# A three-layer graph network on one core: the first layer's neighbour lists are analysed first, and its row gathers are dealt by estimated time

## The chip, the cores and the metric

The kernel runs on one core of a Trainium2 chip. The metric is device time in microseconds (us) of one execution. The engines are named as in the profile: PE (TensorE), DVE (VectorE), ACT (ScalarE), POOL (GpSimd) and SP (the queue that issues most plain DMAs).

## The reference

There are 6250 nodes with 128 features and 200000 edges, sorted by destination. After a layer norm and a ReLU come three layers of the same form (widths 128 to 256, 256 to 256, 256 to 128), and the input is added at the end:

```python
def _sage_conv(x, src, dst, Wl, bl, Wr):
    agg = jax.ops.segment_max(x[src], dst, num_segments=x.shape[0])
    agg = jnp.where(jnp.isfinite(agg), agg, 0.0)
    return agg @ Wl + bl + x @ Wr
h = jnp.maximum(_layernorm(x, axis=-1), 0.0)
for Wl, bl, Wr in layers:
    h = jax.nn.leaky_relu(_sage_conv(h, src, dst, Wl, bl, Wr), 0.01)
return x + h
```

Nearly all work is in `segment_max(x[src], dst)`: for every node, the maximum over its neighbours' rows.

## The kernel before

The nodes form 50 tiles of 127 rows. The neighbours of a node are taken in two ways. Of the neighbours that lie in one pair of source tiles, one (or two) is taken by **lookup**: a one-hot matrix is made from a row of indices and multiplied on PE with the pair of source tiles. What is left over goes to **lists**: at most some tens of neighbours of a node, fetched row by row from the table in DRAM by indirect DMAs that POOL issues (a **gather**: 128 rows of 128 floats in the first layer).

**Steps.** The three layers are written as 1025 steps; the first layer is steps 0 to 224. In the code it is `layer == 0`; the text calls it the first layer. It has three sweeps over the 25 pairs of source tiles: steps 0 to 74 take the lookups of group 0 (three steps for each pair), steps 75 to 124 those of group 1 (two steps for each pair), steps 125 to 224 those of groups 2 and 3 (four steps for each pair). In a step PE makes the products (`products`, L997), and DVE takes the running maximum over them out of PSUM (`maxima`, L1014). The one-hots are made up to six steps ahead. In the first sweep all of them are made on ACT (L967 and L969); in the two others ACT makes one half and DVE the other (L963).

**Chores.** The lists and the index rows have to be made from the edges first. Group 0 and list 0 are done before step 0. For lists 1, 2 and 3 this is work for DVE during the first layer's steps: `late_rows(k)` masks and flags the rows of a list (`mask_rows`, `flag_rows` with `repeated`), picks what is left over (`pick_rows`, L558 and L560) and ranks the rows by their count (`rank_rows`, from L574). POOL then scatters the picked rows, one indirect DMA each (`send_row`, L630), and SP loads the ordered list (`load_ell`). `late_lookups(us, s)` makes the index rows for the lookups (`expand`, L742 to L749, and `lookups`). `spread` deals the chores over the steps in proportion to a cost written by hand.

**Gathers.** `CAPS` says how many gathers each column of a list takes: 118 for list 0, 70, 255 and 110 for lists 1, 2 and 3, so 553 in a layer. 44 of the first layer's are issued before step 0 (`early`). `release` copies four index columns on ACT (`let`, L1035), `gather` issues on POOL (L1046) into a ring of 8 tiles, each of 8 gathers in the first layer, and `maximum` takes the maximum of the tiles on DVE (L1060, then a tree, L1065) and sends a column's result to `best` by a DMA on SP's queue (L1069). Where each stands is set by `plan(step, rank, f)`: every engine takes its instructions in the order of the steps, and within a step in the order of ranks. Before the change the gathers that are left after the early ones are dealt evenly over the layer's steps, and the maximum stands eight steps (four for list 3) behind the gather:

```python
for part, t0, t1 in (((items[:parted], t0, turn), (items[parted:], turn, t1)) if alone else ((items, t0, t1),)):
    ...
    while total[t + 1] <= total[-1] * i / n:
        t += 1
    whens.append(t0 + t)
...
plan(max(whens[i] - LEAD, 0), LET, lambda li=li, t=t: li.release(t))
plan(whens[i], GATHER, lambda li=li, t=t: li.gather(t))
at = max(at, whens[i] + (SOON if k == NL - 1 and not (alone and i < parted) else DELAY[layer]))
plan(at, MAXIMA, lambda li=li, t=t: li.maximum(t))
```

**Nodes.** When a group's sweep and its list are done, each of its tiles is finished (`Node`): POOL fetches the list's maximum (L1089; L1158 for the split rows of group 1), PE transposes it and multiplies by the weights, and the new rows go to the next layer's table. The next layer's gathers begin when the whole table is written.

Of the kernel before, what the change touches and what calls it, by code (L numbers as in the profile page):

```python
# [66 lines left out]
HOT, HOTS, MORE = 1024, 6, 1  # L67
# [5 lines left out]
def kernel(ctx: ExitStack, tc: tile.TileContext, x, src, dst,  # L73
# [32 lines left out]
    LISTS = ([("n", i) for i in range(NEAR)],) + GROUPS[1:]  # L106
# [6 lines left out]
    NL = len(LISTS)  # L113
# [308 lines left out]
    jobs = []  # L422
# [7 lines left out]
    for i in range(NEAR):  # L430
        window(ORDER[i])
        while rest and len(jobs) - 4 - len(rest) <= i * (len(jobs) - 4) / 17:
            stage, b = rest.pop(0)
# [194 lines left out]
    def send_row(k, i):  # L628
        nc.gpsimd.memset(gap_t, 0.0)
        s = nc.gpsimd.indirect_dma_start(  # L630
            out=picks[k], out_offset=bass.IndirectOffsetOnAxis(ap=to_i[k][:, i : i + 1], axis=0),
            in_=picked[k][:, i, :], in_offset=None,
        )
        for j in sent[k]:
            tc.declare_no_dep(s.ins, j.ins, reason="rows are disjoint")
        sent[k].append(s)

    def load_ell(k):
        n = len(LISTS[k])
        nc.sync.dma_start(ell[k], picks[k].rearrange("(p q) m -> p q m", q=n))  # L640
# [217 lines left out]
    for (f, k), s in best.items():  # L858
        n = len(LISTS[k]) * P
# [34 lines left out]
    RING = 8  # L894
# [252 lines left out]
    class Joined:  # L1147
# [27 lines left out]
        def send(self, v):  # L1175
            K, F = self.K, self.F
            p = psum.tile([P, K, P], F32, tag="tr", name="jT_p")
            for i in range(K):
                nc.tensor.transpose(p[:, i, :], self.acc[:, i, v * P : (v + 1) * P], ident)
            t = node.tile([P, H], F32, tag="s", name="joined_v", bufs=2)  # L1180
            nc.scalar.copy(t[:, :F], p.rearrange("p k f -> p (k f)"))
            nc.sync.dma_start(joined[F][v * P : (v + 1) * P, :], t[:, :F])


    steps, begins, ends_at = [], [], {}
# [24 lines left out]
    def plan(t, rank, f):  # L1210
        agenda.setdefault((t, rank), []).append(f)

    LET, TURN, MAXIMA, ROWS, REST, LINEAR, MERGE, SOONER, GATHER, FETCH = range(10)
    LEAD = 2
# [7 lines left out]
    chores = []  # L1222
    here_now, listed_at = [0], {0: 0}

    def late_rows(k):
        us = LISTS[k]
        i0 = 0
        for part in [list(p) for _, p in itertools.groupby(us, key=lambda u: u[0])]:
            chores.append((2.5, lambda part=part: mask_rows(part, S_acc)))
            chores.append((len(part) * (1 if part[0][0] == "w" else .6), lambda part=part: flag_rows(part, S_acc)))  # L1230
            for i in range(0, len(part), 4):
                chores.append((7, lambda k=k, i0=i0 + i, p=part[i : i + 4]: pick_rows(k, i0, p, S_acc)))
            i0 += len(part)
        chores.append((7, lambda: rank_rows(k, S_acc, made)))
        for i in range(0, len(us), 4):
            chores.append((0, lambda i=i: [send_row(k, j) for j in range(i, min(i + 4, len(us)))]))

        def load():
            load_ell(k)
            listed_at[k] = here_now[0]  # L1240

        chores.append((0, load))

    def late_lookups(us, s):
        got = {}
# [5 lines left out]
            chores.append((.7 * len(us), part))  # L1251
        chores.append((2, lambda: lookups(us, got[0], s, made)))

    late_rows(1)
    late_lookups(LISTS[1], 0)
    late_lookups(LISTS[1], 1)
    late_lookups(EXTRA, 0)
    n_soon = len(chores)
    late_rows(2)
    for s in range(2):  # L1260
        late_lookups(LISTS[2][:NW], s)
    rest2 = LISTS[2][NW:]
    cuts = -(-len(rest2) // 8)
    for i in range(cuts):
        late_lookups(rest2[len(rest2) * i // cuts : len(rest2) * (i + 1) // cuts], 0)
    late_rows(3)
    late_lookups(LISTS[3], 0)

    def spread(jobs, t0, t1):
        whole, done = sum(c for c, _ in jobs), 0.0  # L1270
        for c, f in jobs:
            plan(t0 + int((t1 - t0) * done / whole), MAXIMA, f)
            done += c

    spread(chores[:n_soon], 0, 40)
    spread(chores[n_soon:], 40, 82)
    DELAY = (8, 6, 6)
    SOON = 4
    WIDER = (1.0, 1.25, 1.25)
# [2 lines left out]
    for layer in range(3):  # L1282
        b0, end = begins[layer], begins[layer + 1]
        lists_ = [early_list if (layer, k) == (0, 0) else Listed(layer, k) for k in range(NL)]
        early = 0 if layer else EARLY
        turn = ends_at[layer, 2] - DELAY[layer]
        whens = []
        t0, t1 = max(b0 + 2, rows_at), end - 1 - SOON
        alone = len(SWEEPS[layer][-1]) == 1
        items = [(k, t) for k in range(NL) for t in range(len(lists_[k].seq))]  # L1290
        if alone:
            own = [(3, t) for t in range(len(lists_[3].seq))]
            later_n = len(items) * (t1 - turn) / (t1 - t0)
            heads = [t for t, (_, j) in enumerate(lists_[3].seq) if j == 0]
            cut = min(heads, key=lambda t: abs(len(own) - t - later_n))
            mid = next(i for i, (k, _) in enumerate(items) if k == 2)
            items = items[:mid] + own[:cut] + [q for q in items if q[0] == 2] + own[cut:]
            parted = len(items) - (len(own) - cut)
        for part, t0, t1 in (((items[:parted], t0, turn), (items[parted:], turn, t1)) if alone else ((items, t0, t1),)):
            total = [0.0]  # L1300
            for t in range(t0, t1):
                total.append(total[-1] + (WIDER[layer] if steps[t][3][3] is not None else 1.0))
            n = len(part) - early
            whens += [None] * early
            early, t = 0, 0
            for i in range(n):
                while total[t + 1] <= total[-1] * i / n:
                    t += 1
                whens.append(t0 + t)
        done_at, at = [0] * NL, 0  # L1310
        for i, (k, t) in enumerate(items):
            li = lists_[k]
            if whens[i] is None:
                at = 1 + i // 8
            else:
                plan(max(whens[i] - LEAD, 0), LET, lambda li=li, t=t: li.release(t))
                plan(whens[i], GATHER, lambda li=li, t=t: li.gather(t))
                at = max(at, whens[i] + (SOON if k == NL - 1 and not (alone and i < parted) else DELAY[layer]))
            plan(at, MAXIMA, lambda li=li, t=t: li.maximum(t))
            done_at[k] = at  # L1320
        gap = (2, 3, 3)[layer]
        late = 0

        def begin(key, make):
            def f():
                accs[key] = make()
                accs[key].fetch()
            return f

        def stages(ta, key, make, after=(3, 4, 5, 6)):  # L1330
            plan(ta, FETCH, begin(key, make))
            for d, rank, stage in (
                (after[0], MERGE, "merge"), (after[1], LINEAR, "linear"),
                (after[2], ROWS if after[2] > after[1] else SOONER, "rows"), (after[3], TURN, "turn"), (after[3], REST, "rest"),
            ):
# [426 lines left out]
```

## Time and profile before

| | |
|---|---|
| median of 3 runs | 3156.43 us (3152.08 to 3160.95) |
| profiled execution | 3156.75 us, span of the profile 3155.0 us, granted TensorE clock 0.914 |
| busy, of the span | PE 2407.1, DVE 2523.6, ACT 1901.4, POOL 2049.3 us |
| gathers (L1046) | 1659 in three layers, 1697.4 us on POOL |

The first layer's gathers start at 213.7 us and its last step's maxima end at about 1161 us. A row of a view gives the engine, the line, the operation, the tiles (written `<-` read), the count, the busy time with the mean of one, and the idle time ahead of it with what ended that wait. "issue" is idle time for which the profile shows no wait. PE's busy time says little on how hard it works, since matmuls are pipelined; DVE and ACT begin an instruction slightly ahead of the end of the one before, so that single durations add up to a little more than the elapsed time.

### The profile page before, as it was taken

What the parts mean: (1) busy time and instruction counts of PE and PEld (TensorE: products, weight loads), DVE (VectorE), ACT (ScalarE), POOL (GpSimd) and SP (SyncE); (2) the same over time, 40 slices, a digit from 0 to 9 for tenths busy, and PEclk for the clock granted to TensorE, in tenths of its full rate; (3) what the DMA queues carried; (4) which work ended last, traced back from release to release, by engine and by line L of the source; (5) the groups of instructions that cost most, each with busy time, mean ns of one, the idle gap of its engine ahead of it and who ended that gap; (6) DMA issues with size and microseconds to landing.
All of it is one profiled execution on the core that took longest, in us unless ns stands there. A gap on an engine that the chain in (4) does not pass through costs nothing.

```text
span 3155.0 us, 36991 instructions
## 1 busy us (share of the span) xinstructions
PE 2407.1 (76%) x9909; PEld 1806.9 (57%) x9909; DVE 2523.6 (80%) x4059; ACT 1901.4 (60%) x2793; POOL 2049.3 (65%) x2059
## 2 busy tenths in 40 slices
PE   1024643568677569999987899999999996898886
PEld 1023322345455457777775677777777775676665
DVE  7576899889778666899986679995799987799854
ACT  4216963848567556666654567874666664567652
POOL 4787543667777752677776557762477777677662
PEclk9996766779888889999998999999999998999998
DMA  9224541569566657667675676766667676776684
GB/s 299 73 60 117 158 115 54 153 146 283 167 181 179 142 148 243 203 211 216 203 183 173 220 220 209 210 201 211 209 209 219 215 176 177 212 221 205 202 254 148
DMA packets 365615, 585.57 MB, mean 186 GB/s; under 512 B 64588, under 2 KB 216279, under 8 KB 364757
## 3 DMA queue, kind: packets, MB, share of 16 engines
q1 hardware_dynamic: 237141, 336.67, 33.3%
q0 software_dynamic: 84992, 212.22, 27.2%
q10 hardware_dynamic: 43264, 34.21, 3.3%
q8 instruction: 83, 1.36, 0.2%
q14 instruction: 135, 1.11, 0.1%
HBM read 458.31 MB, written 124.54 MB: 185 GB/s over the span
## 4 chain that ended last, share of the span: by engine, by line
PE 33%; DVE 26%; DMA 16%; issue 9%; POOL 7%; ACT 5%; SPq 1%; DVEq 0%; ACTq 0%; POOLq 0%
PE pg L997 25%; DVE acc L1014 11%; DMA g<-table,let 8%; POOL g L1046 6%; PE z_p L1118 3%; DVE g L1065 3%; DVE g L1060 3%; ACT away L967 2%; PE z_p L1120 2%; ACT hot L969 2%; DMA pair_sb<-pair 1%; DVE acc L560 1%; DMA hT_in<-across 1%; DVE acc L558 1%; PE hT_p L872 1%
## 5 line engine op out<-in xcount | busy, mean ns | idle before, releaser
L997 PE MATMUL pg<-hot,pair_sb 128*128 128x512 f32 x8000 | 2113.5, 416 | 383.0 <-DVE acc L1014 108.0
L1046 POOL DMA_INDIRECT g<-table,let x1659 | 1697.4, 1023 | 677.4 <-issue 383.2
L997 PEld LDWEIGHTS pg<-hot,pair_sb 128*128 128x128 f32 x8000 | 1532.9, 200 | 834.9 <-ACT hot L969 229.9
L1014 DVE TENSOR_TENSOR acc<-acc,pg 128x1024 f32<-128x1024 f32 (+2 forms) x1239 | 1434.0, 1182 | 296.0 <-PE pg L997 278.9
L969 ACT ACTIVATE hot<-away 128x1024 fp32r<-128x1024 uint8 (+2 forms) x600 | 574.1, 957 | 350.8 <-PE pg L997 338.4
L969 ACT ACTIVATE hot<-idx_sb 128x1024 fp32r<-128x1024 uint8 (+2 forms) x600 | 555.8, 937 | 232.6 <-PE pg L997 221.9
L967 ACT ACTIVATE away<-idx_sb,near 128x1024 uint8<-128x1024 uint8 (+2 forms) x600 | 620.4, 1034 | 49.9 <-DMA idx_sb<-idx 27.1
L1060 DVE TENSOR_TENSOR g<-g 128x1024 f32<-128x1024 f32 (+5 forms) x247 | 249.3, 1009 | 63.3 <-DMA g<-table,let 56.3
L1089 POOL DMA_INDIRECT agg<-best,end_i x141 | 143.1, 1015 | 213.4 <-PE aT_p L1105 146.9
L1122 ACT COPY s<-z_p 127x256 f32<-127x256 f32 (+1 forms) x150 | 50.2, 335 | 286.0 <-PE z_p L1120 236.1
L1065 DVE TENSOR_TENSOR g<-g 128x256 f32<-128x256 f32 (+3 forms) x357 | 176.9, 496 | 10.5
L1035 ACT ACTIVATE let<-ell 128x4 int32<-128x4 int16 (+3 forms) x477 | 86.5, 189 | 103.2 <-DMA ell<-picks 92.5
L1118 PE MATMUL z_p<-wr,hT_in 128*128 128x256 f32 (+1 forms) x500 | 135.6, 389 | 3.7 <-DMA hT_in<-across 3.7
L630 POOL DMA_INDIRECT picks<-picked,to_i x55 | 56.6, 1029 | 98.4 <-DVE rank_h L606 60.5
L1120 PE MATMUL z_p<-wl,mz 128*128 128x256 f32 (+1 forms) x500 | 117.2, 351 | 2.2 <-DVE mz L1111 2.1
L1111 DVE TENSOR_TENSOR mz<-acc,aT_p 128x256 f32<-128x256 f32 (+1 forms) x141 | 52.4, 372 | 81.5 <-PE aT_p L1105 81.5
L963 DVE TENSOR_SCALAR hot<-idx_sb,beyond 128x1024 fp32r<-128x1024 uint8 (+2 forms) x150 | 108.8, 725 | 0.0
L1120 PEld LDWEIGHTS z_p<-wl,mz 128*128 128x128 f32 x500 | 88.0, 202 | 12.4 <-DVE mz L1111 3.3
L1118 PEld LDWEIGHTS z_p<-wr,hT_in 128*128 128x128 f32 x500 | 80.4, 202 | 24.9 <-DMA hT_in<-across 5.3
L353 POOL DMA_INDIRECT win_d<-in_dst_dram,win_i x50 | 52.3, 1047 | 51.3 <-ACT junk_w L358 22.7
L874 ACT COPY hT<-hT_p 128x254 f32<-128x254 f32 x100 | 36.8, 368 | 72.5 <-PE hT_p L872 71.6
L1105 PE MATMUL aT_p<-ident,agg 128*128 128x128 f32 x250 | 54.4, 284 | 22.7 <-DMA agg<-best,end_i 14.2
(284 smaller groups left out, 1109.7 us busy)
## 6 DMA issues: line engine op xcount, KB each, us to landing
pair_sb<-pair SPq DMA_DIRECT2D x325, 256.0 KB
idx_sb<-far SPq DMA_DIRECT2D x50, 640.0 KB
g<-table,let POOLq DMA_INDIRECT x1659
far<-away ACTq DMA_DIRECT2D x200, 128.0 KB
pair<-pr SPq DMA_DIRECT2D x100, 256.0 KB
idx_sb<-idx SPq DMA_DIRECT2D x75, 320.0 KB
idx_sb<-far SPq DMA_DIRECT2D x50, 320.0 KB
best<-g SPq DMA_DIRECT2D x110, 128.0 KB
```

The costliest lines, as they stand in the source:

```text
L963: nc.vector.tensor_scalar(hot[:, :w], d, beyond, None, op0=OP.is_equal)
L967: nc.scalar.activation(away, d, AF.Abs, bias=near[:, s : s + 1], scale=1.0)
L969: nc.scalar.activation(hot[:, :w], d, AF.Relu, bias=1.0, scale=-1.0)
L997: nc.tensor.matmul(to, pr[:, i, kk * P : (kk + 1) * P], hot[:, o : o + bw], start=((alone or s == 0) and i == 0), stop=((alone or s == 1) ...
L1014: nc.vector.tensor_max(to, to, of)
L1035: nc.scalar.activation(let[:, :n], ell[self.k][:, q, j : j + n], AF.Identity, scale=1.0)
L1046: nc.gpsimd.indirect_dma_start(out=self.tiles[q, b][:, i, :], out_offset=None, in_=tables[self.layer], in_offset=bass.IndirectOffsetOnAxis ...
L1060: nc.vector.tensor_max(base[:, : i + 1, :], base[:, : i + 1, :], g[:, : i + 1, :])
L1065: nc.vector.tensor_max(base[:, :h, :], base[:, :h, :], base[:, w - h : w, :])
L1089: nc.gpsimd.indirect_dma_start(out=self.agg[:, : self.F], out_offset=None, in_=of, in_offset=bass.IndirectOffsetOnAxis(ap=at, axis=0),)
L1118: nc.tensor.matmul(z_p, self.hT[:, i, :], wr[layer][:, i, :], start=False, stop=False)
L1120: nc.tensor.matmul(z_p, self.m[:, i, :], wl[layer][:, i, :], start=False, stop=(i == K - 1))
```

## The change

It touches the first layer alone. First, the rows of all three late lists are analysed in steps 0 to 28, ahead of all late lookups; those of group 1 then stand in steps 29 to 57 and those of groups 2 and 3 in steps 58 to 107 (before: list 1 with its lookups in steps 0 to 39, the rest in steps 40 to 81). Second, the scatter of a list's rows on POOL stands three steps behind its rank, and no longer right behind it. Third, the gathers are dealt by a running clock: `begun` estimates when each step begins from costs written by hand, a gather takes `PACE`, and a gather stands in the first step that has begun by that clock once its list is known and a tile of the ring is free; its maximum stands in the step that begins 25 us later (`LANDS`).

```diff
+    sends_at, HOLD = {}, 3
     def late_rows(k):
...
         chores.append((7, lambda: rank_rows(k, S_acc, made)))
-        for i in range(0, len(us), 4):
-            chores.append((0, lambda i=i: [send_row(k, j) for j in range(i, min(i + 4, len(us)))]))
-        def load():
-            load_ell(k)
-            listed_at[k] = here_now[0]
-        chores.append((0, load))
+        sends_at[len(chores) - 1] = k
...
-    late_rows(1)
+    for k in range(1, NL):
+        late_rows(k)
+    n_rows = len(chores)
     late_lookups(LISTS[1], 0)
...
-    late_rows(2)
...
-    late_rows(3)
...
+    PACE, LANDS = 1.35, 25.0
...
+            if n in sends_at:
+                k = sends_at[n]
+                plan(t + HOLD, MAXIMA, lambda k=k: send(k))
+                listed_from[k] = t + HOLD
-    spread(chores[:n_soon], 0, 40)
-    spread(chores[n_soon:], 40, 82)
+    spread(0, n_rows, 0, 29)
+    spread(n_rows, n_soon, 29, 58)
+    spread(n_soon, len(chores), 58, 108)
+    begun = [0.0]
+    for t in range(begins[1]):
+        _, k, _, (_, w, _, odd_u) = steps[t]
+        wide = odd_u is not None
+        share = w / HOT
+        by_act = share * (4.2 if k == 0 else 2.1)
+        by_dve = share * ((2.4 if wide else 1.2) + (.8 if k else 0)) + work_at[t] + .5
+        begun.append(begun[-1] + max(by_act, by_dve, share * 2.4) + .3)
...
+        if layer == 0:
+            clock, at, top, end_of, rel = 0.0, 1, 0, {}, []
+            free = {k: t + 3 + int(PACE * len(LISTS[k]) / 4) for k, t in listed_from.items()}
+            busy = {t: PACE * len(LISTS[k]) for k, t in listed_from.items() if k}
+            for i, (k, t) in enumerate(items):
...
+                if whens[i] is not None:
+                    at = max(at, free[k] + LEAD if k else 1)
+                    if at_b == 0 and len(rel) > RING:
+                        at = max(at, end_of[rel[-1 - RING]])
+                    clock = max(clock, begun[at])
+                    while at < t1 - 1 and begun[at + 1] <= clock:
+                        at += 1
+                        clock += busy.pop(at, 0.0)
+                    whens[i] = at
+                    clock += PACE
+                    top = max(top, at)
+                    while top < t1 and begun[top] < clock + LANDS:
+                        top += 1
...
+            elif layer == 0:
+                plan(max(whens[i] - LEAD, 0), LET, lambda li=li, t=t: li.release(t))
+                plan(whens[i], GATHER, lambda li=li, t=t: li.gather(t))
+                at = max(at, lands[i], whens[i] + 2)
```

The counts of instructions stay. Counted over the steps, 287 gathers that follow the early ones stand in steps 0 to 74 (before: 171), the last one in step 141 (before: 219), and the last maximum over gathers in step 151 (before: 223). Until the last gather the order puts 617 indirect DMAs on POOL in the first layer: 553 gathers, 35 scatters and 29 fetches for nodes.

POOL's order from the last scatter of list 2 (`picks_161`) over those of list 3 (`picks_162`) to the first fetches for nodes of group 0, before:

```order
L630 DMA picks_161<-picked_856,to_i_860 2560x48
L1046 DMA g<-table_75,let 128x128 x58
L629 MEMSET gap_t 128x1
L630 DMA picks_162<-picked_857,to_i_861 896x40
...
L1046 DMA g<-table_75,let 128x128 x3
L1089 DMA agg<-best_0_140,end_i_850 128x128
L1046 DMA g<-table_75,let 128x128 x2
```

And after:

```order
L630 DMA picks_161<-picked_856,to_i_860 2560x48
L1046 DMA g<-table_75,let 128x128 x13
L629 MEMSET gap_t 128x1
L630 DMA picks_162<-picked_857,to_i_861 896x40
...
L1046 DMA g<-table_75,let 128x128 x186
L1089 DMA agg<-best_0_140,end_i_850 128x128
L1046 DMA g<-table_75,let 128x128 x7
```

The scatters have moved ahead, and 186 gathers now stand between them and the first fetch, where 3 stood.

POOL's order at the end of the first layer, from the last pair of fetches for the split rows (`agg_v`) over the three nodes of the `joined` rows to the nodes of group 2 (`best_2`), before:

```order
L1158 DMA agg_v<-best_1_141,end_i_851 128x128 x2
L1046 DMA g<-table_75,let 128x128 x26
L1089 DMA agg<-joined_148,last_i 128x128
L1046 DMA g<-table_75,let 128x128 x2
...
L1046 DMA g<-table_75,let 128x128 x179
L1089 DMA agg<-best_2_142,end_i_852 128x128 x20
```

And after:

```order
L1158 DMA agg_v<-best_1_141,end_i_851 128x128 x2
L1046 DMA g<-table_75,let 128x128 x23
L1089 DMA agg<-joined_148,last_i 128x128
L1046 DMA g<-table_75,let 128x128 x2
L1089 DMA agg<-joined_148,last_i 128x128 x2
L1089 DMA agg<-best_2_142,end_i_852 128x128 x20
```

The 179 gathers that stood last on POOL in the layer are gone from there.

DVE's order at the end of the layer (one-hots L963, maxima over lookups L1014, the tree of a list's last column L1065), before, up to the last maximum of the layer:

```order
L1014 TENSOR_TENSOR acc_1514<-acc_1514,pg 128x1024 x2
L1065 TENSOR_TENSOR g<-g 128x512
L1065 TENSOR_TENSOR g<-g 128x256
L1065 TENSOR_TENSOR g<-g 128x128
L963 TENSOR_SCALAR hot<-idx_sb,beyond 128x512
L1014 TENSOR_TENSOR acc_1514<-acc_1514,pg 128x1024
L963 TENSOR_SCALAR hot<-idx_sb,beyond 128x896
L1014 TENSOR_TENSOR acc_1514<-acc_1514,pg 128x512
```

And after, from the tree of the same column:

```order
L1065 TENSOR_TENSOR g<-g 128x128
L963 TENSOR_SCALAR hot<-idx_sb,beyond 128x512
L1014 TENSOR_TENSOR acc_1514<-acc_1514,pg 128x1024
L963 TENSOR_SCALAR hot<-idx_sb,beyond 128x896
L1014 TENSOR_TENSOR acc_1514<-acc_1514,pg 128x512
L963 TENSOR_SCALAR hot<-idx_sb,beyond 128x1024
L1014 TENSOR_TENSOR acc_1513<-acc_1513,pg 128x896
...
```

Behind that tree 93 maxima over lookups and 74 one-hots are left for DVE in the layer, about 18.5 pairs of source tiles with five maxima and four one-hots each; before, 3 maxima and 2 one-hots were left.

More of the change, by code (lines that the diff above doesn't have):

```diff
@@ L1265, with send, spread @@
         late_lookups(rest2[len(rest2) * i // cuts : len(rest2) * (i + 1) // cuts], 0)
-    late_rows(3)
     late_lookups(LISTS[3], 0)
[L1269 to L1272, printed above, removed]
-            done += c
-    spread(chores[:n_soon], 0, 40)
-    spread(chores[n_soon:], 40, 82)
+    PACE, LANDS = 1.35, 25.0
+    work_at = [0.0] * len(steps)
+    listed_from = {0: 0}
+    def send(k):
+        for j in range(len(LISTS[k])):
+            send_row(k, j)
+        load_ell(k)
+        listed_at[k] = here_now[0]
+    def spread(n0, n1, t0, t1):
+        whole, done = sum(c for c, _ in chores[n0:n1]), 0.0
+        for n in range(n0, n1):
+            c, f = chores[n]
+            t = t0 + int((t1 - t0) * done / whole)
+            plan(t, MAXIMA, f)
+            work_at[t] += c
+            done += c
+            if n in sends_at:
[13 more added lines that the diff above has]
+        begun.append(begun[-1] + max(by_act, by_dve, share * 2.4) + .3)
     DELAY = (8, 6, 6)
@@ L1309 @@
                 whens.append(t0 + t)
+        lands = [0] * len(items)
+        if layer == 0:
[3 more added lines that the diff above has]
+            for i, (k, t) in enumerate(items):
+                li = lists_[k]
+                q, j = li.seq[t]
+                b, at_b = divmod(j, li.B)
+                if at_b == 0:
+                    rel.append((k, q, b))
+                if whens[i] is not None:
[11 more added lines that the diff above has]
+                        top += 1
+                else:
+                    top = 1 + i // 8
+                lands[i] = end_of[k, q, b] = end_of[k, q, 0] = top
         done_at, at = [0] * NL, 0
```

## The prediction

> **What bounds the kernel now.** I read the page first, for the time against which the sum is made.
>
> ```profile
> span 3155.0 us, 36991 instructions
> PE 2407.1 (76%) x9909; PEld 1806.9 (57%) x9909; DVE 2523.6 (80%) x4059; ACT 1901.4 (60%) x2793; POOL 2049.3 (65%) x2059
> ```
>
> The profiled execution took 3156.75 us, its span is 3155.0, the median of the runs is 3156.43: the sum on the profile can stand for the median. No engine is full over the whole span. The change touches the first layer alone, so I went on to the busy time by stretches there: steps 0 to 74 are about 213 to 646 us (two rows), the second sweep 646 to 838, the third 838 to 1163. The last row counts list gathers and their maxima alone.
>
> ```profile
> 213.00:352.00 139.00, 66.52 (x181) 40.45 (x178) 101.64 (x257) 93.38 (x120) 106.98 (x117) 0.73 0.53 138
> 352.00:646.00 294.00, 145.27 (x397) 90.48 (x398) 261.01 (x808) 200.65 (x254) 138.72 (x159) 0.69 0.40 109
> 646.00:838.00 192.00, 149.02 (x575) 101.29 (x574) 176.10 (x268) 130.15 (x196) 148.87 (x146) 0.92 0.82 227
> 838.00:1163.00 325.00, 212.42 (x736) 155.29 (x735) 235.85 (x325) 193.40 (x272) 245.26 (x239) 0.82 0.60 158
> ...
> 838.00:1163.00 325.00, 41.61 (x81) 230.52 (x224) 0.82 0.60 158
> ```
>
> The columns are PE, PE's weight loads, DVE, ACT, POOL. In the first sweep DVE is full (362.6 of 433 us) and POOL is not. In the third POOL has 245.3 us in 239 instructions; to see whether that is full one has to know what lies between two of them. The groups of POOL's instructions, in 213 to 646 us and then in 646 to 1153:
>
> ```profile
> L1046 POOL DMA_INDIRECT g<-table,let x217 | 214.2, 987 | 95.0 <-issue 50.9 <-ACT let L1035 15.1 <-DVE acc L748 9.1
> L630 POOL DMA_INDIRECT picks<-picked,to_i x28 | 27.8, 994 | 65.7 <-DVE rank_h L606 60.5 <-issue 4.9 <-DVE acc L748 0.2
> L629 POOL MEMSET gap_t<- 128x1 f32 x29 | 3.5, 119 | 0.0
> ...
> L1046 POOL DMA_INDIRECT g<-table,let x336 | 350.3, 1043 | 104.5 <-issue 80.2 <-DMA g<-table,let 9.2 <-ACT let L1035 4.0
> L1089 POOL DMA_INDIRECT agg<-best,end_i x20 | 20.9, 1043 | 6.1 <-issue 3.1 <-PE pg L997 0.6 <-PE z_p L1118 0.6
> L630 POOL DMA_INDIRECT picks<-picked,to_i x7 | 7.3, 1050 | 29.1 <-DVE rank_f L607 28.2 <-issue 1.0
> ```
>
> Between gathers lie 0.30 us of issue (80.2 over 263 of them; the timeline below shows it singly). So a gather costs 0.987 + 0.30 = 1.287 us in the first stretch and (350.3 + 104.5) / 336 = 1.354 in the second, and 336 of these with 20 fetches at 1.35 and some more fetches fill 646 to 1153 us: from the second sweep on, **POOL paces the layer**. In the first sweep it stands idle, 60.5 us in one wait for a rank, with more gathers queued behind it, and 28.2 more just behind. The layer's gathers run from here to here:
>
> ```profile
> L1046 POOL DMA_INDIRECT g<-table,let x217: 940/944/1909, 213.7 to 618.3; - x109
> ...
> L1046 POOL DMA_INDIRECT g<-table,let x336: 938/945/2259, 657.1 to 1151.9; - x168
> ```
>
> The waits agree (213 to 646 us above, 838 to 1163 below): DVE waits for gathers to land in the third sweep, and little for PE.
>
> ```profile
> ACT let L1035 <- DMA ell<-picks: 23.7, 1, 23.7
> ...
> DVE g L1060 <- DMA g<-table,let: 34.5, 7, 10.5
> ...
> DVE acc L1014 <- PE pg L997: 22.2, 27, 2.6
> ```
>
> **The change part by part.** Nothing is added or removed: 553 gathers, 35 scatters, the same chores. What moves is where POOL is idle.
>
> Rows first, scatters three steps later: POOL comes to the scatter of list 2 behind 149 indirect DMAs, at about 213.7 + 141 x 1.287 + 8 x 1.29 = 405 us. DVE has then to have passed the rank in step 20. The picks of the three lists cost it little more than 75 us (the two rows below with their loads), and with them the 60.5 and 28.2 us on POOL and the 23.7 us on ACT go. I cost what is left of these waits at nothing; cover is the three steps, and the rival on a starved POOL has the price if that is too little.
>
> ```profile
> L558 DVE MAX8 acc<-acc 128x8 f32<-128x64 f32 (+1 forms) x155 | 35.9, 245 | 4.5
> L560 DVE MATCH_REPLACE8 acc<-acc,acc 128x64 f32<-128x64 f32 (+1 forms) x120 | 27.7, 231 | 0.0
> L560 DVE MATCH_VALUE_LOAD acc<-acc,acc 128x8 f32 x120 | 11.1, 92 | 4.1
> ```
>
> Lookups later: they move behind the rows and reach to step 107; group 2's first step is 125, so I let nothing wait for them. On DVE the first sweep loses the lookups of steps 75 to 107 and gains maxima over 116 more gathers, 116 x 41.61 / 224 = 22 us by the row of the third sweep. Even without the loss its 433 us become 455, and POOL will need 471, as follows: nothing on the path. The index copies on ACT and the columns' `best` stores on SP's queue move with their gathers. A store waits there for DVE's tree, and the pair and index loads behind it on the queue wait too, as they do before the change: nothing new, while SP stays ahead by its four pair tiles.
>
> Gathers by the clock: 331 of the 553 now stand up to step 74, and none behind step 141. They are still 617 indirect DMAs on one queue that starts at 213.7 us. The price of a scatter is (27.8 + 3.5 + 4.9) / 28 = 1.29. The sum: 331 x 1.287 = 426.0 and 35 x 1.29 = 45.2 bring POOL to 684.9 us at the end of the first sweep, where before DVE came to it at 646. Then 222 x 1.354 = 300.6 and 29 fetches x 1.35 = 39.2: the last gather is issued at 1024.7. The landing and the tree behind it are taken from the chain of waits near the end of the layer:
>
> ```profile
> 1145.58 2.48 DMA g<-table,let
> 1148.06 0.75 DVE g L1065
> ...
> 1148.84 0.44 DVE g L1065
> ...
> 1149.29 0.36 DVE g L1065
> ```
>
> That is 4.0 us: DVE passes step 151 at **1028.7**. All maxima and one-hots behind that tree stand behind it on DVE, so the 18.5 pairs of tiles that are left can't begin earlier. What a pair costs without gathers no row shows alone. The timeline of the third sweep has a rhythm, from one one-hot of 896 to the next but one:
>
> ```profile
> 961.00 0.67 DVE L963 TENSOR_SCALAR hot<-idx_sb,beyond 128x896 fp32r<-128x896 uint8 x1
> ...
> 963.92 0.74 DVE L963 TENSOR_SCALAR hot<-idx_sb,beyond 128x1024 fp32r<-128x1024 uint8 x1
> 964.12 1.36 POOL L1046 DMA_INDIRECT g<-table,let  x1 [0.30 <-issue]
> ...
> 965.78 0.94 POOL L1046 DMA_INDIRECT g<-table,let  x1 [0.30 <-issue]
> ...
> 966.98 1.47 DVE L1065 TENSOR_TENSOR g<-g 128x512 f32<-128x512 f32 x3
> ...
> 969.89 0.68 DVE L963 TENSOR_SCALAR hot<-idx_sb,beyond 128x896 fp32r<-128x896 uint8 x1
> ...
> 973.59 1.47 DVE L1065 TENSOR_TENSOR g<-g 128x512 f32<-128x512 f32 x3
> ...
> 979.44 0.73 DVE L963 TENSOR_SCALAR hot<-idx_sb,beyond 128x896 fp32r<-128x896 uint8 x1
> ```
>
> Two pairs in 18.44 us, less two trees of 1.47: 7.75 a pair, or 143 us for 18.5. From above: DVE's 235.85 us less 41.61 for gathers, and its 22.2 of waits for PE, over 25 pairs: 8.66, or 160. I take 8.0, nearer to the two pairs, since some waits for PE are themselves made by late one-hots: **148 us**. Bounds 137 (7.4, the first of the two pairs) to 160.
>
> So the layer's maxima end at 1028.7 + 148 = 1176.7. Before they end here:
>
> ```profile
> 1160.10 0.68 DVE L963 TENSOR_SCALAR hot<-idx_sb,beyond 128x896 fp32r<-128x896 uint8 x1
> 1160.69 0.68 DVE L1014 TENSOR_TENSOR acc<-acc,pg 128x512 f32<-128x512 f32 x1
> ```
>
> At 1161.4, so 15.3 us later. What follows, from the nodes of groups 2 and 3 on, stands in the same order as before and moves with it: 3156.75 + 15.3 = **3172 us**, 0.5% more. In words: before, POOL idles at the start of the layer; after, it idles through the last 73 steps, and that is the longer of the two.
>
> How far the pace of the gathers can be trusted decides this. In the timeline above a gather beside a one-hot of DVE takes 1.36 us, one beside maxima out of PSUM 0.94. The Trainium skill, SBUF — State Buffer, section "Who interferes with whom", has one rule for this: DVE and GpSimd share a port pair under an exclusive lock, and a DVE instruction with at most one SBUF input outside the two-port modes leaves it alone. The two gathers agree. By that rule the gathers moved into the first sweep, where DVE makes no one-hots, could all go at 0.94 + 0.30: 331 x 0.042 = 14 us less, and the forecast would be 3158. I stay with the row's mean, 0.987, since it was taken in that very sweep, beside the chores.
>
> **The rivals.** *Faster: the gathers go at their floor.* With 0.945 + 0.30 = 1.245 us for each of the 582 gathers and fetches, 45.2 for the scatters and 7.75 a pair, the layer ends at 213.7 + 724.6 + 45.2 + 4 + 143 = 1130.5: 3126 us. For it speaks that the median gather in both stretches takes 0.944 to 0.945, and that DVE is less crowded in steps 75 to 151, when it waits for POOL. Against it, no long stretch shows that mean. The sign turns at a mean of (1161.4 - 148 - 4 - 213.7 - 45.2) / 582 = 1.290 us, where my sum has 1.316; for 0.3% less it takes 1.273.
>
> *No change.* Between 1.273 and 1.306 us a gather the two idle times cancel within 0.3%, about what a measurement of this kernel can tell from no change. 3157 us.
>
> *Slower: POOL starves in the dense part.* All picks and ranks fall into steps 0 to 28, on DVE, which frees the ring's 8 tiles in the same order; where POOL is ahead there, it waits for a tile, an index copy or a rank. One such wait was 60.5 us. Every idle us of POOL before step 141 is an us of the end. At 40 us the time is 3212. Against it: POOL comes to the scatter of list 2 only at 405 us by the sum above, some 190 us into the layer, of which the picks take 75 on DVE.
>
> That the change does not do what it says I rule out by the order: POOL's gathers do move.
>
> **How the numbers follow.** Chances: forecast 0.40 (its own range 3161 to 3190, from 137 and 160 us for the tail and a few us of pace), starved 0.17, no change 0.16, floor 0.27. Faster by over 0.3%: 0.27; within: 0.16; slower: 0.57. The range runs from 3130, near the floor's end, to 3212.
>
> **What would show it.** Right: in the trace after, POOL without waits for ranks in 213 to 650 us, the last gather of the first layer near 1025 us, a DVE that waits for gathers in the second sweep, and some 150 us of layer behind it in which POOL has next to nothing. Wrong: a last gather well before 1000 us; DVE without waits for gathers in the second sweep; a tail of over 170 us; or layers two and three of another length.

## The result, and the profile after

The changed kernel takes 3207.66 us (median of 4 runs, 3200.98 to 3214.27); the kernel before took 3158.69 in the runs beside it. The ratio is **1.0162** (95% interval 1.014 to 1.0185): 49 us slower, where the prediction had 15.

The page of the profile after, its span, busy times and POOL's row of the 40 slices (80 us each):

```profile
span 3199.1 us, 37017 instructions
...
PE 2408.7 (75%) x9909; PEld 1805.9 (56%) x9909; DVE 2522.8 (79%) x4059; ACT 1902.1 (59%) x2793; POOL 2039.3 (64%) x2059
...
POOL 4787677777777001477777557772277777677672
```

Busy times are those of before within 0.5%: no work came or went, so the 44 us of span are idle time. POOL's row has it: sixes to eights from the second slice to the 13th, and then two slices of zero. In the windows below steps 0 to 74 are the first row, the second sweep the second, the third sweep the last two:

```profile
213.00:677.00 464.00, 213.99 (x550) 133.35 (x550) 357.65 (x1003) 288.71 (x396) 347.15 (x377) 0.67 0.51 123
677.00:967.00 290.00, 178.06 (x588) 117.61 (x589) 212.07 (x390) 138.64 (x221) 220.09 (x218) 0.78 0.64 174
967.00:1067.00 100.00, 59.16 (x219) 41.79 (x218) 64.02 (x92) 48.88 (x70) 62.58 (x63) 0.81 0.52 146
1067.00:1214.00 147.00, 129.22 (x524) 96.94 (x523) 139.98 (x173) 138.76 (x151) 0.00 (x0) 0.98 0.53 165
```

DVE, full in the first sweep of before (362.6 of 433 us), now has the same work in 464 us. The second sweep grew from 188 to 290 us, and there no engine but POOL is full: its 218 instructions with 0.30 us between them make 285 us. In the last 147 us of the layer POOL does nothing at all, and DVE and ACT are full.

POOL's groups from 213 to 677 us, and from 677 to 1044:

```profile
L1046 POOL DMA_INDIRECT g<-table,let x307 | 308.5, 1005 | 110.1 <-issue 71.3 <-DMA g<-table,let 9.6 <-DVE acc L578 8.5
L630 POOL DMA_INDIRECT picks<-picked,to_i x35 | 34.6, 988 | 6.6 <-issue 6.3 <-DVE acc L558 0.2
...
L1046 POOL DMA_INDIRECT g<-table,let x245 | 247.4, 1010 | 78.3 <-issue 57.3 <-DMA g<-table,let 12.2 <-ACT hot L969 2.1
L1089 POOL DMA_INDIRECT agg<-best,end_i x21 | 21.6, 1028 | 6.4 <-issue 4.0 <-PE z_p L1118 0.6 <-DVE acc L748 0.3
L1158 POOL DMA_INDIRECT agg_v<-best,end_i x8 | 7.9, 986 | 2.4 <-issue 1.8 <-DMA agg_v<-best,end_i 0.3 <-PE vT_p L1167 0.3
```

The waits for ranks, 60.5 and 28.2 us before, are gone from the scatters (6.6 us of idle for 35 of them, 6.3 of it issue). The last gather, from the view of the tile:

```profile
L1046 POOL DMA_INDIRECT g<-table,let x552: 940/944/2891, 213.3 to 1039.6; - x184
...
  DVE acc L578: 8.5, 1
  DVE g L1065: 8.2, 3
```

(The first of the 553 began at 212.0 us, ahead of the window. The two rows below are POOL's waits that the profile puts down to a chore of DVE and to a tree of DVE, which frees a tile of the ring.) The last gather is issued at 1039.6 us, 112 us earlier than before, and the layer ends later all the same: at 1213.9 the first product of step 225 starts, at 1162.5 before. That is 51 us; layers two and three, from there to the last product, take 1949.0 us in place of 1954.8 (1949 to 1967 us in the kernels of the table below).

### The profile page after: what moved, and what is told of

It is laid out like the page before. It is cut to its first block, busy times and chain, and to the rows that moved or that the text cites. A ratio compares the mean times of both kernels' runs of the same rounds, so it can differ in the third digit from the quotient of the medians.

```text
span 3199.1 us, 37017 instructions
## 1 busy us (share of the span) xinstructions
PE 2408.7 (75%) x9909; PEld 1805.9 (56%) x9909; DVE 2522.8 (79%) x4059; ACT 1902.1 (59%) x2793; POOL 2039.3 (64%) x2059
## 4 chain that ended last, share of the span: by engine, by line
PE 31%; DVE 25%; DMA 17%; issue 9%; POOL 7%; ACT 5%; SPq 0%; DVEq 0%; ACTq 0%; POOLq 0%
PE pg L997 23%; DVE acc L1014 11%; DMA g<-table,let 10%; POOL g L1046 7%; PE z_p L1118 3%; DVE g L1065 3%; DVE g L1060 3%; ACT away L967 3%; PE z_p L1120 2%; DMA far<-away 2%; ACT hot L969 2%; DMA pair_sb<-pair 1%; DVE acc L560 1%; DVE acc L558 1%; PE hT_p L872 1%
## 5 line engine op out<-in xcount | busy, mean ns | idle before, releaser
L1014 DVE TENSOR_TENSOR acc<-acc,pg 128x1024 f32<-128x1024 f32 (+2 forms) x1239 | 1434.4, 1182 | 286.4 <-PE pg L997 268.6
L967 ACT ACTIVATE away<-idx_sb,near 128x1024 uint8<-128x1024 uint8 (+2 forms) x600 | 620.3, 1034 | 91.6 <-DMA ell<-picks 45.0
L1060 DVE TENSOR_TENSOR g<-g 128x1024 f32<-128x1024 f32 (+5 forms) x247 | 249.3, 1009 | 79.8 <-DMA g<-table,let 74.2
L1065 DVE TENSOR_TENSOR g<-g 128x256 f32<-128x256 f32 (+3 forms) x357 | 177.1, 497 | 13.8 <-DMA g<-table,let 3.1
L874 ACT COPY hT<-hT_p 128x254 f32<-128x254 f32 x100 | 36.8, 368 | 128.4 <-PE hT_p L872 126.5
L963 DVE TENSOR_SCALAR hot<-idx_sb,beyond 128x1024 fp32r<-128x1024 uint8 (+2 forms) x150 | 105.9, 706 | 0.0
L1105 PEld LDWEIGHTS aT_p<-ident,agg 128*128 128x128 f32 x250 | 35.8, 145 | 71.3 <-issue 26.4
```

The source lines that it names most:

```text
L963: nc.vector.tensor_scalar(hot[:, :w], d, beyond, None, op0=OP.is_equal)
L967: nc.scalar.activation(away, d, AF.Abs, bias=near[:, s : s + 1], scale=1.0)
L1014: nc.vector.tensor_max(to, to, of)
L1060: nc.vector.tensor_max(base[:, : i + 1, :], base[:, : i + 1, :], g[:, : i + 1, :])
L1065: nc.vector.tensor_max(base[:, :h, :], base[:, :h, :], base[:, w - h : w, :])
L1105: nc.tensor.transpose(aT_p[:, i, :], self.agg[:, i * P : (i + 1) * P], ident)
```

## The experiments

All are edits of the changed kernel unless said otherwise. The places are read from the traces: the start of a step's first product, the issue of the first layer's last gather, and what is left of the layer from there to the start of step 225, in us of the profiled execution.

| kernel | median us | ratio to before (95%) | step 75 | step 125 | last gather | left | step 225 |
|---|---|---|---|---|---|---|---|
| before | 3158.69 | | 646 | 834 | 1152 | 11 | 1162.5 |
| after | 3207.66 | 1.0162 (1.014-1.0185) | 677 | 967 | 1040 | 174 | 1213.9 |
| e1, even deal of before | 3134.99 | 0.9937 (0.9917-0.9956) | 612 | 825 | 1132 | 10 | 1142.3 |
| e2, new deal alone | 3188.46 | 1.0107 (1.0082-1.0132) | 685 | 914 | 1142 | 43 | 1185.0 |
| e3, no hold | 3217.00 | 1.0204 (1.0182-1.0225) | 679 | 969 | 1043 | 176 | 1218.7 |
| e4, even by time | 3112.63 | 0.9864 (0.9841-0.9886) | 646 | 865 | 1096 | 20 | 1115.9 |
| e7, maxima later | 3167.56 | 1.0028 (1.0012-1.0043) | 668 | 910 | 1081 | 92 | 1173.0 |
| e8, gather at 1.75 | 3114.90 | 0.9868 (0.9836-0.9900) | 639 | 866 | 1081 | 37 | 1117.6 |
| e12, merges later | 3211.82 | 1.0177 (1.0146-1.0207) | 679 | 974 | 1045 | 174 | 1218.1 |
| e5, after halved | 3023.93 | 0.9577 (0.9547-0.9607) | 609 | 817 | 853 | 184 | 1037.0 |
| e6, before halved | 3021.44 | 0.9563 (0.9533-0.9593) | 619 | 799 | 1009 | 25 | 1033.4 |

**The parts of the change, e1 to e4.** e1 keeps the rows first and the later scatters, and deals the gathers evenly over the steps as before:

```diff
-        if layer == 0:
+        if False:
...
-            elif layer == 0:
+            elif False:
```

> The rows first and the scatters three steps behind their ranks, but the gathers dealt evenly over the steps as in the kernel before (171 of them in steps 0 to 74 behind the early ones, the last in step 219). Theory (the order of POOL's indirect DMAs paces the layer, and the change moves POOL's idle time from the layer's start to its end): POOL's waits for ranks of 60.5 and 28.2 us go, the first sweep gets shorter by some 30 to 50 us since lookups leave it, and the rest stays paced by POOL at some 500 us: 3107 to 3130 us, faster than before. Rival A (the rows first crowd DVE in steps 0 to 28 and that is what costs): slower than before by some 40 us, near 3200. Rival B (the three steps and the rows are worth nothing, all is in the deal of the gathers): 3157, as before.

e2 does the reverse, the new deal with the chores in their old places and the scatter right behind its rank:

```diff
-    sends_at, HOLD = {}, 3
+    sends_at, HOLD = {}, 0
...
-    for k in range(1, NL):
-        late_rows(k)
-    n_rows = len(chores)
+    late_rows(1)
...
-    spread(0, n_rows, 0, 29)
-    spread(n_rows, n_soon, 29, 58)
-    spread(n_soon, len(chores), 58, 108)
+    spread(0, n_soon, 0, 40)
+    spread(n_soon, len(chores), 40, 82)
```

> The gathers dealt by the running clock as in the changed kernel, but the chores in the order and steps of the kernel before and the scatters right behind their ranks. Theory: the lists come late, so the clock deals the gathers later and POOL still waits for the ranks of lists 2 and 3; the last gather is nearer to the layer's end than in the changed kernel: 3150 to 3200 us, not slower than the changed kernel. Rival A (rows first cost): as before or faster, 3120 to 3157, since DVE is not crowded. Rival B (the deal is the cost): 3200 or more.

e3 is the changed kernel with `HOLD = 0` alone, the scatter planned right behind its rank. (The planner then also puts 42 gathers some steps earlier, all of them before step 32; the last one stays in step 141.)

> The changed kernel with the scatters right behind the ranks in place of three steps later. Theory: POOL then reaches the scatters of lists 1 and 2 ahead of the ranks and waits 5 to 15 us in each, and each us of idle POOL is an us of the end: 3210 to 3235 us. Rivals A and B: no difference, 3208.

e4 is e1 with the even deal weighted by what a step takes in the three sweeps of before:

```diff
-                total.append(total[-1] + (WIDER[layer] if steps[t][3][3] is not None else 1.0))
+                total.append(total[-1] + ((5.1 if t < 75 else 4.2 if t < 125 else 2.75) if layer == 0 else WIDER[layer] if steps[t][3][3] is not None else 1.0))
```

> Rows first and scatters three steps behind, and the even deal weighted by how long a step takes: 5.1 for steps 0 to 74, 4.2 for 75 to 124, 2.75 from 125 on, so that POOL gets its gathers evenly over time, to the end of the layer. Theory: POOL idles neither at the start nor at the end; 619 indirect DMAs at 1.30 to 1.34 us from 213 us end at 1018 to 1043 us, and DVE with 774 us of work and some waits ends near 1090: 3070 to 3100 us, the fastest. Rival A (rows first cost): 3180 or more. Rival B (dealing more gathers into the first sweep is the cost, here 225 of them): between before and after, 3165 to 3185.

The loss is the deal's. Rows first with the old deal are 0.6% faster than before (5 us above the range expected), the deal with the old chores 1.1% slower, both together 1.6%. The parts don't add up, because e2's deal is not the deal of after: its lists are known later, so the same clock puts 214 gathers into steps 0 to 74 and the last one into step 198, where after has 287 and step 141 (counted over the plan's steps). So rows first brings the gathers forward and makes the deal's tail longer. The rows of POOL's waits, e1's and then e2's:

```profile
POOL picks L630 <- DVE rank_h L606: 32.7, 1, 32.7
...
POOL picks L630 <- DVE rank_h L606: 94.4, 1, 94.4
```

Before, the same wait was 60.5 us. With three steps of distance but the old deal (e1) POOL still waits 32.7 us for a rank; e3, with no distance, keeps POOL's scatters free of such waits:

```profile
L630 POOL DMA_INDIRECT picks<-picked,to_i x35 | 35.5, 1013 | 6.5 <-issue 6.1 <-DVE least L749 0.2 <-DVE sums L621 0.2
```

So in after it is not the hold that took the waits away, but the early ranks together with the gathers that stand ahead of the scatters: POOL comes late. e3's time lies in the range that I gave to its theory, but by luck: the waits that it named did not come. What the hold itself is worth, 9 us by the medians, is no more than suggested, since the intervals overlap. e4 missed its expectation by 13 us, but has the same first two parts as after, a deal weighted by time too, and takes 95 us less: a deal by time is not the fault, only how early this one is.

**Is it POOL's queue? e5 and e6.** In after and in before each column of the first layer's lists keeps only the first half of its gathers; those that are kept stay in their places.

```diff
+            self.caps = [(m + 1) // 2 if layer == 0 else m for m in CAPS[k]]
...
-            if j % self.n:
+            if j % self.n or j >= self.caps[q]:
...
+            if j >= self.caps[q]:
+                return
```

> After, with the first layer's gathers halved in place: each column of a list keeps only the first half of its gathers, and every one that is kept stays where it was (so half of the first layer's list neighbours are left out). Theory (POOL's queue paces the first layer after step 75, and the changed deal only moves its idle time to the end): with some 275 gathers fewer POOL is no longer full, the 52 us by which the first layer is longer are gone, and this kernel and the halved before are within 1% of each other, both some 60 to 200 us below the full before, 2950 to 3100. Rival A (rows first crowds DVE, or later lookups delay the second sweep; the gathers have nothing to do with it): after stays 40 to 50 us above the halved before. Rival B (the ranks and list loads are what before loses by): it is 30 us or more below the halved before.

> Before, with the first layer's gathers halved in place in the same way (half of the first layer's list neighbours are left out). Theory: the third sweep is POOL's at the even deal, 245 of 325 us busy; with half the gathers it is bound by DVE and PE, near 8 us a pair as in the tail of after, so 25 pairs take some 200 us in place of 325, and the time is 2950 to 3100. Rival A: 3100 to 3150, as the third sweep is bound by something else and the gathers were hidden.

3023.93 and 3021.44 us: the two are equal within their intervals. The window from 800 to 1034 us, first of after halved (its third sweep is 817 to 1037), then of before halved (799 to 1033):

```profile
800.00:1034.00 234.00, 199.33 (x780) 141.41 (x778) 212.31 (x274) 196.59 (x229) 32.69 (x31) 0.96 0.58 169
...
800.00:1034.00 234.00, 190.08 (x738) 136.34 (x737) 214.62 (x304) 191.31 (x250) 128.54 (x121) 0.94 0.65 187
```

POOL has 33 us of work in the one and 129 in the other, and neither is full; the fullest engine is DVE, with 212 and 215 of 234 us, and it no longer matters when the gathers come. The idle time of POOL at the end costs nothing by itself: after halved has 184 us left behind its last gather and is no slower. So the order of the chores does not cost the 49 us, and without a full POOL the deal costs nothing. (The third sweep of e6 takes 235 us, not some 200 as I had written: 9.4 us a pair.)

**Where the gathers and their maxima stand, e7 and e8.** The planner's two numbers, one at a time:

```diff
-    PACE, LANDS = 1.35, 25.0
+    PACE, LANDS = 1.35, 50.0
```

> After, with the maxima over gathers planned 50 us behind their gather by the planner's clock in place of 25. Theory (POOL's queue paces; the maxima wait only because POOL is late, and the merges of nodes wait for fetches that stand behind gathers in the same queue, which this edit doesn't move): 3195 to 3215, no difference beyond 0.4%. Rival (the planner's lag is too short, and DVE's waits for gathers hold up PE and the sweep): 3160 to 3185.

```diff
-    PACE, LANDS = 1.35, 25.0
+    PACE, LANDS = 1.75, 25.0
```

> After, with the planner's price of a gather 1.75 us in place of 1.35, so that the same gathers are dealt over more steps of the three sweeps. Theory (what costs is that the plan puts all gathers before step 142 and POOL reaches them late, with the last 75 steps left without any): the last gather moves towards the last steps, POOL's idle tail becomes shorter, and the time falls between after and the kernel whose even deal is weighted by time: 3120 to 3170. Rival (rows first crowds DVE in the first sweep, the deal hardly matters): 3195 to 3215.

e8 came out as the theory said, below its range's lower end. e7 didn't: 40 us faster than after, the price of its rival. I had overlooked that a gather may not stand before its tile of the ring is free by the plan, in the step of an earlier maximum: with later maxima the gathers move too, the last one from step 141 to 180 and its maximum from 151 to 199 (counted over the plan's steps). It is no test of the lag alone. The last gathers of e7 and e8:

```profile
L1046 POOL DMA_INDIRECT g<-table,let x552: 940/944/2890, 212.9 to 1081.1; - x184
...
L1046 POOL DMA_INDIRECT g<-table,let x552: 938/945/2872, 212.9 to 1080.6; - x184
```

POOL is done at the same time in both, and e8's layer still ends 55 us earlier: when POOL issues the last gather, PE is at step 183 of 224 in e7 and at step 209 in e8 (at 141 in after). The end of the layer is the last gather plus the steps that are left, and the deal sets both.

**What holds the steps behind POOL? e9 and e12.** In after the steps behind 75 wait for two things that POOL's queue brings late. The waits in 650 to 1044 us:

```profile
PE aT_p L1105 <- DMA agg<-best,end_i: 46.0, 13, 19.0
...
DVE mz L1111 <- PE aT_p L1105: 42.1, 10, 13.4
...
PE vT_p L1167 <- DMA agg_v<-best,end_i: 24.9, 5, 19.8
...
DVE g L1060 <- DMA g<-table,let: 18.5, 4, 7.6
```

These are node fetches (70.9 us of PE's time) that stand behind gathers, and gathers themselves (18.5 us of DVE's). e9 and e12 are one kernel: the merges of the first layer's nodes of groups 0 and 1 are planned further behind their fetches. The fetches are spread too, those of the split rows one a step and not two, and the nodes one in two steps, so that the later of them also stand later on POOL.

```diff
-                    plan(t0 + v // 2, FETCH, lambda key=key, v=v: accs[key].fetch(v))
-                    plan(t0 + 2 + v // 2, MERGE, lambda key=key, v=v: accs[key].merge(v))
+                    plan(t0 + (v if layer == 0 else v // 2), FETCH, lambda key=key, v=v: accs[key].fetch(v))
+                    plan(t0 + (4 + v if layer == 0 else 2 + v // 2), MERGE, lambda key=key, v=v: accs[key].merge(v))
...
-            every = 1 if last or layer == 0 or k in (1, 3) or ends_at[layer, k] == end else 2
+            wait_more = layer == 0 and k < 2
+            every = 2 if wait_more else 1 if last or layer == 0 or k in (1, 3) or ends_at[layer, k] == end else 2
...
-                stages(t0 + every * j, key, make, (2, 3, 3, 4) if last else (3, 4, 5, 6))
+                stages(t0 + every * j, key, make, (2, 3, 3, 4) if last else (8, 9, 10, 11) if wait_more else (3, 4, 5, 6))
```

> After, with the merges of the first layer's nodes of groups 0 and 1 planned further behind their fetch (8 steps in place of 3, one node in two steps; 4 in place of 2 for the split rows). The gathers stay where they are. Theory (in after the steps stand at 142 and not at 151 when the last gather is issued, because PE's transposes wait for node fetches that stand in POOL's queue behind gathers, 71 us of waits in 650 to 1044 us): those waits go, the steps reach about 150 by the last gather, the stretch from there to the end of the layer falls from 174 to 155 to 162 us, and the time is 3180 to 3198. Rival (the steps are held by the gathers themselves, and the merges only show it): the same step stands at the last gather, DVE then waits for gathers instead, 3200 to 3215.

> The kernel with the later merges once more, since in its first run all kernels, before too, stood still some 540 us longer with no cause that the profile names. Theory (the node fetches behind gathers hold PE's transposes, and through them the steps): PE's 71 us of waits for fetches in 650 to 1044 us are gone, the steps reach about 150 by the last gather, what is left of the layer then takes 155 to 162 us in place of 174, and the time is 3180 to 3198. Rival (the gathers themselves hold the steps): DVE waits for gathers instead, and the time is 3200 to 3215.

The waits of e12 in the same stretch:

```profile
DVE g L1060 <- DMA g<-table,let: 36.2, 9, 7.9
...
PE vT_p L1167 <- DMA agg_v<-best,end_i: 19.5, 4, 13.1
...
PE aT_p L1105 <- DMA agg<-best,end_i: 10.1, 3, 7.5
```

The theory falls. PE's waits for fetches go from 70.9 to 29.6 us, DVE's for gathers double, and yet step 125 begins at 974 us (in after at 967), the last gather and the step at it stay (1044.6 us, step 142 in place of 141), and so does the time. The waits did not vanish, they moved: in 677 to 967 us PE now stands 54.9 us for DVE's part of the nodes (`hT_p` for `mz`), where after has 15.5. With POOL full in the second sweep, I read the waits for nodes there as the place where POOL's lateness showed and not as a cost beside it. What this does not settle is the single wait for the split rows, 19.8 us in after between steps 127 and 128 and still 13.1 in e12. No run with this deal and all its gathers is without it; with the later deals the longest wait of PE for these rows is 17.3 us in e7 and 2.9 in e8.

**Three runs under other conditions.** e9, e10 and e11 ran together, and every execution there, of before too (3697.40 us), took some 540 us longer, mostly with engines idle for causes that the profile does not name; so they stand only against each other. e10 is `PACE, LANDS = 1.6, 35.0`, e11 is `PACE, LANDS = 1.75, 50.0`.

> After, with the planner's price of a gather 1.6 us in place of 1.35 and the maxima planned 35 us behind in place of 25 (last gather in step 185, last maximum in step 199). Theory (what decides is POOL's pace up to the last gather and the work left behind it): last gather near 1065 us with some 40 steps left, 80 us, so the layer ends near 1145 and the time is 3125 to 3150, above the kernel with 1.75. Rival (the 1.35 kernel loses by late maxima only, so a lag of 35 is enough): 3105 to 3118.

> After, with 1.75 us as the planner's price of a gather and maxima planned 50 us behind their gather (last gather in step 220). Theory: POOL has slack and DVE hardly waits for gathers with 1.75 and 25 already, so the longer lag brings little: 3105 to 3122. Rival (DVE still loses by late gathers there): 3085 to 3100.

Their ratios are 1.0184 (1.0152 to 1.0215, e9), 1.0142 (1.0110 to 1.0174, e10) and 1.0094 (1.0051 to 1.0136, e11). Only e9 and e11 are apart, the later deal again the cheaper one; the times that were expected can't be read from them, and whether 50 us of lag help at 1.75 stays open.

**The fastest.** e4 and e8 beat both kernels, 3112.63 and 3114.90 us, 1.4 and 1.3% below before and 3% below after; which of the two is better these runs don't tell.

## Why the prediction was right, and what it missed

The direction held, and so did the mechanism: POOL's idle time moves to the end of the layer and is the longer of the two there. The size did not: 15 us were forecast and 49 came. 3207.66 us lies outside the forecast's own 3161 to 3190 and inside the whole range only because its upper end, 3212, was set for a rival, a POOL that starves for 40 us; that the time falls there is luck, since starving is the smaller part of what came. One of my four signs of being wrong came too, a tail of over 170 us: 174 us are left behind the last gather. And DVE's waits for gathers in the second sweep, which I had named as a sign of being right, are small: 18.5 us in 650 to 1044 us, while PE waits 70.9 us for node fetches. Step by step:

**POOL paces the layer, its idle time only moves.** Right: e5 and e6 show it, and so do the two empty slices of the page. The waits for ranks went, as said. ACT's wait for list loads didn't: it was 23.7 us once, and now, in 213 to 650 us,

```profile
ACT away L967 <- DMA ell<-picks: 45.0, 3, 23.6
```

by this row the three loads, each behind its scatters, block ACT's one-hots instead of an index copy. So a term that I had let go to nothing nearly doubled. What of it reaches POOL no run shows; POOL's own waits in this sweep are in the next part.

**The last gather: 1024.7 predicted, 1039.6 measured.** The first sweep is the term that was too small. Its last gather, the 331st, was to be done at 684.9; it was issued at 705.9, 21 us later. By the row of 213 to 677 us a gather there took 1.005 us and not 0.987, and POOL also waited 8.5 us for what the profile calls a chore of DVE and 7.9 of the 8.2 us for tiles of the ring, where I had written these waits at nothing; the starved POOL was a rival at 40 us, and less than half of that came. The rest, 222 gathers and 29 fetches, took 333.7 us in place of 339.8: 1.33 and not 1.354. The floor is refuted: from 212.0 to 1039.6 us, less 45.2 for the scatters, the 582 other DMAs took 1.344 us each, and it needed less than 1.273. By the rule of the Trainium skill, SBUF — State Buffer, section "Who interferes with whom", as I drew on it, the moved gathers could all have gone at 0.94, as DVE makes no one-hots there. The traces agree with the rule itself: in 213 to 677 us, the 22 gathers that ran beside maxima out of PSUM alone took 0.944 us on average, and the 44 that ran beside no instruction of DVE 0.945. What was wrong is my use of it. One-hots are not the only instructions of DVE that hold gathers up: the trees and some of the chores read two operands from SBUF, and such instructions the rule doesn't clear. In the same stretch, gathers that ran beside the int16 chores of L748 alone, which take the minimum of two halves of a tile, took 1.165 us on average (19 of them).

**Where the tail begins.** This is the step that failed most: "DVE passes step 151 at 1028.7", the last gather plus 4.0 us. Step 151 began at 1068.4, 28.8 us behind the last gather. I had let DVE wait at the last maximum for the last gather; but the steps stood at 141 when that gather was issued, ten short of it, and these ten took 28.8 us. DVE did not wait for the last gather at all: it came to the tree of that column at 1069.05 us, with no idle time ahead of it.

```profile
1069.05 1.47 DVE L1065 TENSOR_TENSOR g<-g 128x512 f32<-128x512 f32 x3
```

Why the steps were ten short: from step 127 to 131, 970.9 to 1010.8 us, PE has the merges of the split rows, whose fetches stand on POOL behind the gathers of these very steps. The first of these waits, 19.8 us at step 127, is a good part of the ten steps, by the timeline of PE:

```profile
968.64 2.97 PE L997 MATMUL pg<-hot,pair_sb 128*128 128x512 f32 x11
991.41 0.47 PE L1167 MATMUL vT_p<-ident,agg_v 128*128 128x128 f32 x1 [19.80 <-DMA agg_v<-best,end_i]
```

That this stall put the steps back is argued from the timeline, not shown: e12 made it shorter and other waits longer, and the step at the last gather stayed. So the cause of these 25 us stays open in part. e8 shows that they come with the deal: there the last gather is issued at step 209, and the plan has the last maximum in step 220.

**The tail itself.** 18.5 pairs from 1068.4 to the last maximum at 1213.5 are 145.1 us, 7.84 a pair; predicted 8.0, 148. Right.

The sum closes: 14.9 us for the last gather, 24.8 for the place where the tail begins (28.8 less 4.0), and 2.9 less for the tail make 1176.7 + 36.8 = 1213.5, the measured end of the layer's maxima.

## What to carry to other kernels

Where one queue paces a stretch, its last instruction is not the end: the end is that instruction plus all that is left behind it, and work of the queue that is moved forward only moves its idle time there. Deal such work so that it ends with the stretch, and spread it by the time that the steps take (e4 against e1): the same 553 gathers, dealt over the whole layer and not over its first two thirds, were worth 95 us. A wait that disappears in an experiment is a cost only if the time goes with it; look where it went.

## What was not expected of the hardware

In the runs of e9 to e11, before took some 540 us longer on its one core than in all others, and the profiles don't name the cause. In e11 the mean duration of DVE's maxima was 1184 ns and in the profile of before shown above 1182, but the idle time ahead of them was 776.2 us and not 296.0; e11's row first, then that of before:

```profile
L1014 DVE TENSOR_TENSOR acc<-acc,pg 128x1024 f32<-128x1024 f32 (+2 forms) x1239 | 1443.2, 1184 | 776.2 <-PE pg L997 371.0 <-remote 259.5 <-issue 90.7
...
L1014 DVE TENSOR_TENSOR acc<-acc,pg 128x1024 f32<-128x1024 f32 (+2 forms) x1239 | 1434.0, 1182 | 296.0 <-PE pg L997 278.9
```

PE's products were longer as well, 434 ns on average against 416, at a granted clock of 0.861 against 0.914, but that is 130 us of busy time and not 540. What "remote" stands for in a program on one core these runs don't show.
